# Moving the bookkeeping of a mixture-of-experts router by half a step to a step in a decoder layer's hand-written order

## The chip, the cores and the metric

The kernel runs on 1 core of one Trainium2 chip. Its time is the device time of one execution in microseconds (us). Before the change: 553.12 us, the median of 3 runs (552.07 to 553.45). A core has five engines with queues of their own, each of which works in order: TensorE (PE in the profile; PEld are its weight loads), VectorE (DVE), ScalarE (ACT), GpSimd (POOL), and SyncE (SP), which here only issues DMAs.

## The reference

One decoder layer on x (16 sequences of 128 rows, 256 wide), with a residual around each of three parts:

```python
x = x + attn(layernorm(x))          # latent attention: 16 heads, q of width 72, causal softmax,
                                    #   keys = values = layernorm(x) @ latent_w + latent_b
x = x + birwkv(layernorm(x), ctx)   # sigmoid(r) * (weighted sums of ctx, forth and back in time)
x = x + ffn(layernorm(x))           # 8 experts, the top two of each row, weighted
```

The last part takes logits (2048 rows by 8), picks the two largest of each row, forms the weights of the pair, and adds for each expert `weight * (silu(x @ w_gate.T) * (x @ w_up.T)) @ w_down.T` to the rows that chose it.

## The kernel before

The work is one list of steps, written out by hand. Steps 0 to 63 are the attention: step s is sequence b = s // 4 and head group s % 4 (4 heads of 16). Steps 64 and on are the experts' slots, one slot of 128 rows a step (36 slots, and 3 that are run only if needed).

An attention step issues the scores (L442), the row maxima on DVE (nm, L459), the exps on ACT (L467), and in the next step the reciprocal of the sums (rsum, L479, DVE) and the product with it (pr, L480, POOL). Two steps after its scores the probabilities are transposed (pt, L486), copied out by ACT (aT, L488) and multiplied by the values (py, L494). Query tiles of the next pair of sequences (pq, L404), the output projection (po, L520) and the second part's work for earlier sequences fill the step. I write nm(26) for the maxima issued in step 26, and pt(26) for the transposes issued in step 26; pr(24) is the product for the scores of step 24.

A step has five places: "pre", "A", "B", "C", "D" (L1243, L1246, L1259, L1278, L1283). `at(step, place, fn)` puts an extra piece of work into one. The manual schedule keeps this order, so the order of the places is the order in each engine's queue. "pre" follows the rsum and pr of the step before; "A" follows the transposes; "B" stands behind the new query matmuls and ahead of the values; "C" stands behind the copies of the query tiles, and in a slot behind `up`; "D" is last, in a slot behind `turn` and `down`.

Pieces that the change and the prediction touch:

- `route(r)` (L666): the routing of four sequences, a generator in five parts and then eight scatters. Part 1 (L681 to L691) and part 2 (L684 to L689) find the first and the second expert on DVE; part 3 (L694 to L700) makes sel, d and kp on DVE and one exp on ACT; part 4 (L705 to L723) counts with five small matmuls pf on TensorE and makes the weights g on DVE and the entries on POOL; part 5 (L726 to L737) makes the places on DVE. The scatters (L741) are issued by POOL. Rounds 0, 1 and 2 begin with sequences 3, 7 and 11; round 3 has an order of its own.
- The mix (`mix_1`, `mix_2`, L602 to L609) reads the transposed sums pw from a PSUM bank that pt needs, and POOL adds the result to x. Then statistics (L305), shift (nb_c, L320), the row (L625), its transposes (px, L640), their copy x2T (L645), and the logits pl (L652).
- The scans (L545, L562) and POOL's products kv, S and sums S<-S,bw (L536, L537, L557) belong to the second part. `residual` (L573) ends the first.
- `first_table(0)` (L869) is made after sequence 7 in six parts from the counts pc (L758): whole, share, and four parts of `table` (L773). SP then loads the table (L842) and its list entries. `last_table` (L883) is made in seven parts during slots 11 to 13.
- A slot j gathers its rows (xr, L912), copies two weights (w, L934: one on ACT, one on DVE), turns xr (pxr, L942) into xT (L944), and makes two products s and pu (L980), sl (L990, ACT), hT (L992, DVE), pd (L1002) and y (L1013, DVE), which POOL adds to the output by a DMA (L1018). In the step of slot j the order is: w of j+1, s and pu of j, hT of j, place "C", xT of j+1, pd and y of j-1, place "D".

Of the kernel before, what the change touches and what calls it, by code (L numbers as in the profile page):

```python
# [19 lines left out]
B = 16  # L20
T = 128
N = B * T
C = 256
# [56 lines left out]
def decoder_kernel(  # L80
# [950 lines left out]
    def at(step, place, fn, *args):  # L1031
        plan.setdefault((step, place), []).append((fn, args))
# [107 lines left out]
    for b in range(B):  # L1140
        s = NHG * b
        if b + 1 < B:
            at(s + 2, "pre", load_ctx, b + 1)
        at(s + 1, "C", wkv_exps, b)
        at(s + 2, "B", wkv_back, b)
        at(s + 3, "A", wkv_back_add, b)
        at(s + 4, "B", wkv_forth, b)
        at(s + 5, "A", wkv_forth_add, b)
        at(s + 5, "B", project, b, (0, 1))
        at(s + 6, "B", project, b, (2, 3))  # L1150
        at(s + 6, "C", rest_values, b)
        at(s + 7, "B", project, b, (4, 5))
        at(s + 7, "C" if b < B - 1 else "B", project, b, (6, 7, NP))
        for name, (step, place) in {B - 2: last_but_one, B - 1: last}.get(b, usual).items():
            at(s + step, place, stages[name], b)
        if b < E:
            for k in range(3):
                at(s + 11 + k, "C", load_expert, b, k)
        if b % RB == RB - 1:
            r = b // RB  # L1160
            parts = ((13, "B"), (13, "C"), (14, "B"), (15, "B"), (15, "C"))
            if b == B - 1:
                parts = ((12, "B"), (12, "D"), (13, "B"), (13, "D"), (14, "B"))
            for step, place in parts:
                at(s + step, place, route_part, r)
            for k in range(2 * RB):
                if b < B - 1:
                    at(s + 16 + k, "A", route_part, r)
                else:
                    at(s + 14 + (k + 1) // 3, "CDA"[(k + 2) % 3 if k > 1 else k], route_part, r)  # L1170
        if b + 1 in FIRST_B:
            i = FIRST_B.index(b + 1)
            parts = [(18 + k, "C") for k in range(6)]
            if i:
                parts = [(18, "C"), (20, "D"), (21, "B"), (21, "D"), (22, "D"), (23, "D")]
            for step, place in parts:
                at(s + step, place, table_part, i, first_table, i)
            for k in range(0, S1[i], 2):
                at(s + 24 + k // 2, "C", list_slots, min(2, S1[i] - k))
        if b == B - 1:  # L1180
            for k in range(7):
                at(s + 15 + k // 3, "ABD"[k % 3], table_part, "2", last_table)
            for k in range(0, S2, 4):
                at(s + 17 + k // 4, "C", list_slots, min(4, S2 - k))
            for k in range(4):
                at(s + 20 + k, "B", table_part, "3", very_last)
            for k in range(0, S3, 4):
                at(s + 24 + k // 4, "C", list_slots, min(4, S3 - k))
# [153 lines left out]
```

## Time and profile before

| what | us |
|---|---|
| median of 3 runs | 553.12 |
| the profiled execution, its own time | 554.7 |
| its span, first to last instruction | 553.0 |
| TensorE busy | 512.8 (93%) |
| DVE, ACT, POOL busy | 330.6, 329.3, 327.1 |
| mean granted TensorE clock | 0.984 |

The page's second part cuts the span into 40 equal slices and gives the busy tenths of each:

```profile
PE   4889999999999999999998989999989999989990
...
DVE  3354776687887678888769776555644533333330
ACT  1788998898797888888986873434313232313200
POOL 5356647564787774697646976454875454541532
PEclk9999999999999999999998999999989999999996
```

The attention lasts for about 24 slices, to some 320 us, with DVE and ACT at seven to nine tenths; in the slots after it TensorE is nearly alone. PEclk is the granted TensorE clock: it was at half of full speed from 296.8 to 300.2 us and from 406.0 to 409.4.

The timeline's rows give start, length, engine, line, operation, tiles and shapes, and in brackets how long the engine had been idle before it and what ended that. The ends of matmuls are modelled. Waits name the one who came last.

### The profile page before, as it was taken

What the parts mean: (1) busy time and instruction counts of PE and PEld (TensorE: products, weight loads), DVE (VectorE), ACT (ScalarE), POOL (GpSimd) and SP (SyncE); (2) the same over time, 40 slices, a digit from 0 to 9 for tenths busy, and PEclk for the clock granted to TensorE, in tenths of its full rate; (3) what the DMA queues carried; (4) which work ended last, traced back from release to release, by engine and by line L of the source; (5) the groups of instructions that cost most, each with busy time, mean ns of one, the idle gap of its engine ahead of it and who ended that gap; (6) DMA issues with size and microseconds to landing.
All of it is one profiled execution on the core that took longest, in us unless ns stands there. A gap on an engine that the chain in (4) does not pass through costs nothing. (4 is left out here: it accounts for less than half of the span.)

```text
span 553.0 us, 10138 instructions
## 1 busy us (share of the span) xinstructions
PE 512.8 (93%) x3272; PEld 439.2 (79%) x3272; DVE 330.6 (60%) x831; ACT 329.3 (60%) x953; POOL 327.1 (59%) x379
## 2 busy tenths in 40 slices
PE   4889999999999999999998989999989999989990
PEld 3768787887777887877875679989979999989980
DVE  3354776687887678888769776555644533333330
ACT  1788998898797888888986873434313232313200
POOL 5356647564787774697646976454875454541532
PEclk9999999999999999999998999999989999999996
DMA  5432245364365545131121113232234232325321
GB/s 149 98 88 67 70 133 170 121 198 120 110 182 133 170 130 178 41 98 37 52 79 56 40 53 66 38 65 45 40 40 51 48 51 47 51 47 173 58 30 19
DMA packets 39662, 47.59 MB, mean 86 GB/s; under 512 B 14136, under 2 KB 31416, under 8 KB 39576
## 3 DMA queue, kind: packets, MB, share of 16 engines
q1 hardware_dynamic: 30106, 37.20, 23.0%
q0 software_dynamic: 7936, 9.51, 11.2%
q8 instruction: 28, 0.46, 0.3%
q10 hardware_dynamic: 1566, 0.21, 0.3%
q14 instruction: 26, 0.21, 0.2%
HBM read 28.22 MB, written 13.31 MB: 75 GB/s over the span
## 5 line engine op out<-in xcount | busy, mean ns | idle before, releaser
L467 ACT ACTIVATE pr<-s,nm 128x128 f32<-128x128 f32 x256 | 90.7, 370 | 9.7 <-DVE nm L459 9.5
L480 POOL TENSOR_TENSOR pr<-pr,rsum 128x512 f32<-128x512 f32 x64 | 75.7, 1183 | 33.5 <-DVE rsum L479 25.6
L990 ACT ACTIVATE sl<-s 128x512 f32<-128x512 f32 x36 | 21.5, 598 | 120.7 <-PE s L980 104.9
L1018 POOL DMA_INDIRECT acc<-y,en x28 | 47.5, 1697 | 60.4 <-DVE y L1013 29.8
L442 PEld LDWEIGHTS s<-kvT,q 72*128 72x128 f32 x512 | 65.7, 191 | 18.7 <-issue 12.6
L980 PEld LDWEIGHTS s<-xT,w 128*128 128x128 f32 x576 | 70.5, 195 | 9.4 <-issue 6.7
L980 PE MATMUL s<-xT,w 128*128 128x128 f32 x576 | 72.0, 279 | 5.4 <-DVE xT L944 2.3
L520 PE MATMUL po<-outw_sb,yP 128*128 128x256 f32 x288 | 74.4, 385 | 0.6 <-DMA yP<-yd 0.6
L442 PE MATMUL s<-kvT,q 72*128 72x128 f32 x512 | 70.5, 279 | 3.2 <-DMA q<-qr 2.2
L980 PE MATMUL pu<-xT,w 128*128 128x128 f32 x576 | 70.5, 276 | 0.0
L992 DVE TENSOR_TENSOR hT<-sl,pu 128x512 f32<-128x512 f32 x36 | 24.7, 687 | 74.1 <-PE pu L980 56.9
L1002 PE MATMUL pd<-wall,hT 128*128 x288 | 68.0, 379 | 0.0
L494 PE MATMUL py<-aT,kvN 128*72 128x512 f32 x128 | 66.4, 600 | 1.6 <-ACT aT L488 1.3
L980 PEld LDWEIGHTS pu<-xT,w 128*128 128x128 f32 x576 | 67.7, 193 | 0.0
L404 PE MATMUL pq<-xnT,wq_sb 128*128 128x256 f32 x256 | 65.3, 387 | 0.0
L520 PEld LDWEIGHTS po<-outw_sb,yP 128*128 128x128 f32 x288 | 54.0, 193 | 13.1 <-issue 5.2
L459 DVE TENSOR_REDUCE nm<-s 128x4 f32<-128x512 f32 x64 | 43.6, 682 | 30.5 <-PE s L442 30.5
L1002 PEld LDWEIGHTS pd<-wall,hT 128*128 128x128 f32 x288 | 52.0, 190 | 5.6
L467 ACT ACTIVATION_READ_ACCUMULATOR pr<-s,nm 128x1 f32 x256 | 53.0, 207 | 0.0
L488 ACT COPY aT<-pt 128x512 f32<-128x512 f32 x64 | 37.2, 581 | 26.0 <-PE pt L486 24.6
L404 PEld LDWEIGHTS pq<-xnT,wq_sb 128*128 128x128 f32 x256 | 46.2, 195 | 5.0 <-issue 0.2
L912 POOL DMA_INDIRECT xr<-xn,en x36 | 37.4, 1040 | 13.3 <-issue 7.6
(172 smaller groups left out, 877.8 us busy)
## 6 DMA issues: line engine op xcount, KB each, us to landing
wall<-in_wg_dram SPq DMA_DIRECT2D x8, 512.0 KB
wall<-in_wu_dram SPq DMA_DIRECT2D x8, 512.0 KB
wall<-in_wd_dram SPq DMA_DIRECT2D x8, 512.0 KB
q<-q SPq DMA_DIRECT2D x16, 224.0 KB
yP<-yB SPq DMA_DIRECT2D x32, 112.0 KB
cx<-in_cx_dram SPq DMA_DIRECT2D x16, 128.0 KB
acc<-x SPq DMA_DIRECT2D x16, 128.0 KB
xn<-row SPq DMA_DIRECT2D x16, 128.0 KB
```

The lines of the kernel that those rows point to most:

```text
L404: nc.tensor.matmul(pq[:, :GT], w[:, c, :], xnT[g][:, c, :], start=(c == 0), stop=(c == NC - 1))
L442: nc.tensor.matmul(ps[:, j, :], q[g, hg][0:L, j, ts(i, T)], kvT[g][:, ts(i, T)], start=False, stop=(j == HG - 1), skip_group_check=n >= 2,)
L459: nc.vector.tensor_reduce(nm, ps, AX.X, ALU.max, negate=True)
L467: nc.scalar.activation(pr[:, j, :], ps[:, j, :], AF.Exp, bias=nm[:, j : j + 1], accum_out=sums[:, j : j + 1],)
L480: nc.gpsimd.tensor_mul(pr, pr, rsum.unsqueeze(2).to_broadcast([P, HG, T]))
L488: nc.scalar.copy(aT, pt)
L494: nc.tensor.matmul(py[:L], kvN[g][:, ts(i, L)], aTs.pop((b, hg)), start=True, stop=True)
L520: nc.tensor.matmul(pos[b][:, :C], yP[b][:, i, :], outw_sb[:, i, :], start=(i == 0), stop=(i == NP))
L912: nc.gpsimd.indirect_dma_start(out=xr, out_offset=None, in_=xn2[0 : t["rows"], :], in_offset=bass.IndirectOffsetOnAxis(ap=entries[j][:, 0: ...
L980: nc.tensor.matmul(o[:, ts(f, P)], w[:, c * F + f * P : c * F + (f + 1) * P], xT[:, c, :], start=(c == 0), stop=(c == NC - 1),)
L1002: nc.tensor.matmul(pd[:, :C], hT[:, f, :], wall[:, bass.ds(e, 1), WD0 + f * C : WD0 + (f + 1) * C], start=(f == 0), stop=(f == NF - 1),)
L1018: nc.gpsimd.indirect_dma_start(out=acc if j < SF + S2 else out2, out_offset=bass.IndirectOffsetOnAxis(ap=en[:, 1:2], axis=0), in_=y, in_of ...
```

## The change

Three sets of places are moved; no operation is added or dropped.

```diff
         if b % RB == RB - 1:
             r = b // RB
-            parts = ((13, "B"), (13, "C"), (14, "B"), (15, "B"), (15, "C"))
+            parts = ((14, "B"), (14, "C"), (15, "B"), (15, "C"), (16, "pre"))
             if b == B - 1:
                 parts = ((12, "B"), (12, "D"), (13, "B"), (13, "D"), (14, "B"))
...
             i = FIRST_B.index(b + 1)
-            parts = [(18 + k, "C") for k in range(6)]
+            parts = [(19 + k, "C") for k in range(6)]
             if i:
                 parts = [(18, "C"), (20, "D"), (21, "B"), (21, "D"), (22, "D"), (23, "D")]
...
             for k in range(7):
-                at(s + 15 + k // 3, "ABD"[k % 3], table_part, "2", last_table)
+                at(s + 15 + k // 3, "BCD"[k % 3], table_part, "2", last_table)
```

In the order of the built kernels this becomes: in rounds 0, 1 and 2 parts 1 and 2 stand behind the mix and the next step's maxima instead of ahead of them; part 3 one set of maxima later, with its exp behind the next step's exps on ACT; part 4's matmuls behind py instead of ahead of po; part 5 behind the next rsum. In step 46's place the counts pc stand in step 47, behind the transposes pxn, and each later part of the first table a step later. In slot 11 the share of the last table goes from ahead of the copy of w to between hT and xT; in slot 12 five operations (L801 to L807) do the same. POOL and SP keep their order; ACT's only move is the exp.

## The prediction

> **What bounds the kernel now.** I read the page first, then who TensorE waited for, then the busy time of stretches, then the timeline at each place the diff touches. Times are from the span's start.
>
> ```profile
> PE 512.8 (93%) x3272; PEld 439.2 (79%) x3272; DVE 330.6 (60%) x831; ACT 329.3 (60%) x953; POOL 327.1 (59%) x379
> ```
>
> TensorE sets the pace; a change counts only through TensorE's waits. The waits of PE:
>
> ```profile
> PE s L980 <- DVE xT L944: 2.3, 2, 2.1
> PE pt L486 <- POOL pr L480: 2.3, 2, 1.5
> ...
> PE pt L486 <- DVE m L684: 1.3, 2, 0.7
> ...
> PE pc L758 <- ACT q L410: 1.0, 1, 1.0
> ```
>
> All four stand where the diff moves something. In the timeline they are 0.68 and 0.67 us in routing rounds 0 and 1 (137.8, 215.1), 1.50 in round 2 (295.3), 1.04 at the first table (239.0), 2.14 in the last table (405.6); a fifth, pf after ACT q, is 0.2 twice. Next the stretches (columns: length, busy time of PE, PEld, DVE, ACT, POOL, granted clock, DMA):
>
> ```profile
> 132.40:148.60 16.20, 15.32 (x91) 12.27 (x90) 14.18 (x45) 12.89 (x43) 9.28 (x14) 1.00 0.36 129
> 293.37:296.79 3.42, 1.92 (x19) 1.73 (x17) 3.32 (x13) 2.44 (x11) 1.99 (x4) 1.00 0.30 83
> 296.79:300.20 3.41, 3.41 (x8) 2.13 (x9) 3.34 (x8) 2.52 (x11) 3.41 (x5) 0.50 0.00 0
> ```
>
> Over a whole routing round VectorE (DVE) is 14.18 of 16.20 us busy: there it is nearly a second bound. The last two rows show that the 1.50 us wait is followed by 3.41 us at half clock. Then the timeline of round 0:
>
> ```profile
> 137.79 0.77 POOL L609 TENSOR_TENSOR x<-x,r 128x256 f32<-128x256 f32 x1 [4.14 <-DVE m L684]
> 137.79 0.63 PE L486 MATMUL pt<-ident,pr 128*128 128x128 f32 x4 [0.68 <-DVE m L684]
> 138.00 0.60 DVE L687 TENSOR_TENSOR oh<-oh,rev 128x32 f32<-128x32 f32 x1
> ...
> 149.06 0.68 DVE L459 TENSOR_REDUCE nm<-s 128x4 f32<-128x512 f32 x1
> ...
> 149.65 0.41 DVE L645 COPY x2T<-px 128x256 f32<-128x256 f32 x1
> ...
> 151.36 0.51 PE L652 MATMUL pl<-rw_sb,x2T 128*128 128x8 f32 x4
> ```
>
> L687 takes 0.19 us alone and 0.60 here: it ends as the POOL operation that began before it ends. L689, L694 and L711 do the same (0.43, 0.88, 0.87). Reductions, and operations with an operand in PSUM, do not. So a routing operation behind a POOL product costs up to that product's length (0.75 to 1.05). x2T ends 1.3 us before pl needs it: that is the slack of nm(28), which precedes it.
>
> **Rounds 0 and 1, worked on round 0 (steps 25 to 28; scores begin at 131.88, 136.01, 140.84, 147.65).** Removed: the seven operations of part 1 (1.32 us) ahead of the mix at 133.67. The mix ends at 136.32 instead of 137.64, so pt(26) is free at once: TensorE gains 0.68, and 0.21 more as pf no longer follows pq directly. nm(26) comes at 137.15 instead of 139.49, with DVE idle for 0.35.
>
> Added: the same seven now stand behind nm(26), from 137.8. The earlier mix releases POOL's x, kv, S and pr (0.75, 0.72, 0.72, 1.05) back to back from 136.5 to 139.8, so L681, L686 and L687 wait for one product each: part 1 takes 2.7 instead of 1.3. Statistics and scan (2.0) and part 2 (1.1) follow; nm(27) is at 143.45 (now 143.50). So nothing is won there, but part 3, done by then before, is still to do. sel (L694) waits behind pr of step 26 until 144.7, L697 behind S<-S,bw (L557) until 145.7, kp is ready at 146.3. ACT's L700 has ended its exps and mask at 146.3 and runs at 146.4; the new wait is that L711 stands right behind, on DVE, until 146.7 (behind it: g, rsum(27), part 5, nm(28)). g and rsum follow until 147.5; then part 5, 1.28 plus about 0.8 since L730 meets pr(27), until 149.4; residual and statistics 1.2. nm(28) is at 150.6, **1.57 later than 149.06**.
>
> On TensorE pf comes to its place at 144.1 and waits for sel until 144.7; s(28) starts at 147.2, 0.47 ahead. But x2T ends at 151.63, so pl waits until 151.8 and s(29) is 0.4 late. ScalarE (ACT) runs its exps 1.5 late in steps 28 to 30, the mix of step 29 follows 1.35 late, and POOL's pr(29) (159.61 to 161.56, with pt(31) just behind it at 161.61) ends near 162.9. **Cost +1.35 per round**, after the 0.88 won. TensorE has no spare time to win it back. Ends: −0.9 (all stalls gone, nothing new), +1.6. The scatters L741 stand behind rs_b at 149.98 and their place is ready at 149.5: free.
>
> **The first table with round 1.** pc waits for ACT q because both banks hold pq(5) and pq(6) of a step with two tiles; a step later one tile is made and the bank is free: −1.04. But pt(47), now at 240.19, needs pr(45), which ended at 238.82 and comes 1.35 later with round 1, at 240.2. So the 1.04 only hides in the delay of round 1: the pair costs +0.3 (pc's own 0.25 moved behind pt, little else), up to 0.65 if the yP load of step 47 is late too; I take **+0.5**, ends −1.9 and +1.0. Of the other parts, the last stands in step 52 ahead of rsum(52) and delays it from 266.9 to 268.0, ahead of nm(53) at 268.4; SP's load of the table is at 268.7, so the list DMAs on SP behind it stay. Without that cover 1.0.
>
> **Round 2.** No query tiles remain, a step is about 4 us, and DVE has 3.32 of 3.42 filled. The wait of 1.50 and the half clock go. The same chain then gives nm(59) at 296.6 (now 297.75), sel behind pr(58) at 297.95, while TensorE stands before pf from 296.0: a **new wait of 2.0**. nm(60) follows at 303.9 (303.06 now), pl waits 1.05 for x2T, and py(61), held by ACT, starts at 308.35 (307.82). **+0.55**, ends −2.7 and +1.6.
>
> Here a rule and a row differ. The Trainium skill, "TensorE: Matmul & The Clock Gate", section "Why this matters for your kernels", puts the drop to half clock at gaps of about 3 us. In this trace a wait of 1.50 was enough, in a stretch filled with transposes and pf. By the rule the old wait has cost 1.5 and the new one of 2.0 costs only itself; by the row the old one has cost 1.5 + 1.7, and the new one may bring another half-clock stretch, which lies where TensorE waits 0.6 + 1.05 anyway. I follow the row; the end of this sum is set by ACT's chain either way.
>
> **The last table.** Slot 11: the five share operations (393.83 to 394.68) lie now in idle time ahead of hT. They go between hT (to 396.77) and xT, which ends at 398.04 instead of 397.10; s at 397.75 moves by 0.44. Slot 12: five operations (1.2 us) leave the place before the copy of w and go between hT and xT.
>
> ```profile
> 404.41 0.69 DVE L992 TENSOR_TENSOR hT<-sl,pu 128x512 f32<-128x512 f32 x1 [1.13 <-PE pd L1002]
> ...
> 405.01 0.42 DVE L944 COPY xT<-pxr 128x256 f32<-128x256 f32 x1
> ...
> 405.58 3.35 PE L980 MATMUL s<-xT,w 128*128 128x128 f32 x16 [2.14 <-DVE xT L944]
> ```
>
> DVE was free for hT at 403.3; it waited on to 404.4 for TensorE's signal, though pu shows its end at 401.5. Elsewhere hT starts 0.11 after pu. If the signal is as late again, s comes at 407.3: +1.7. If not, hT is at 402.25, the five operations to 404.15, s at 404.7, and the half clock after it goes: −0.9 − 1.7 = −2.6. The nearest row is the 0.11 of the other slots, but the profiled execution (554.7, span 553.0) is 1.6 above the median of the runs, so they have probably lacked that signal's lateness already. Against the median I take **0**. Parts moved from A to B, where slots have nothing between, change no order.
>
> **Sum.** 1.35 + 0.5 + 0.55 + 0 = +2.4: 555.4 of span, 557.1 as profiled; on the median 553.1 + 2.4 = **555.5**.
>
> **Rivals.** First: the stalls go and DVE keeps up. For it: each wait removed is on TensorE, and DVE is free for a while ahead of rounds. Against it: 14.18 of 16.20. Sum −0.9 − 0.9 − 1.04 − 1.0 + 0.2 = −3.6: 549.5. It decides if nm(28) is no later than 150.3, the slack before pl. Second: half of it, DVE's part 1 slips between POOL's products: rounds near 0, table −1, round 2 about +0.5, last table +0.2: 553, no change. My forecast is the slower one; its mechanism is DVE's queue between nm(27) and nm(28), price 1.57, and its opposite is the first rival.
>
> **Numbers.** Slower chain 0.54, the even case 0.23, stalls gone 0.23. What can be told from no change is 0.3% (1.7 us). The range reaches from 550.0 (most of the rival's case) to 558.0 (last signal late again, both rounds at their upper ends). The slower case's own range is 554.0 to 558.0.
>
> **What would show it.** Right: nm(28) 1 to 2 us later against s(25) than the present 17.2; pl waiting for x2T; pf waiting for DVE; pt after the round waiting for POOL pr; pc without wait, and a new wait at pt in the same step. Wrong: no wait at pl, or L687 and L694 at 0.19; then the first rival holds. In the last table, hT 0.11 after pu or late again.

## The result, and the profile after

| | median | runs |
|---|---|---|
| before | 552.27 us (550.71 to 553.45) | 7 |
| after | 555.38 us (554.51 to 555.93) | 7 |

The ratio is 1.0045, with a 95% interval of 1.003 to 1.006: after is slower, by 3.1 us where 2.4 were forecast. Yet the two profiled executions have almost the same span, 553.0 and 552.8. Their traces show why: the profile of before holds one accident of 2.8 us. The profiled execution took 554.7 us, longer than each of the seven runs of before, so these probably lacked it. First the page of after, its line of busy times:

```profile
PE 512.3 (93%) x3272; PEld 437.8 (79%) x3272; DVE 334.4 (60%) x831; ACT 328.6 (59%) x953; POOL 327.1 (59%) x379
```

TensorE does the same work; VectorE (DVE) is busy for 3.8 us more with the same 831 instructions. So they last longer on the average. Who TensorE waited for in after (columns: sum in us, times, longest):

```profile
PE pf L705 <- DVE sel L694: 3.3, 3, 1.8
PE pt L486 <- POOL pr L480: 2.7, 3, 0.9
...
PE pl L652 <- DVE nr L581: 1.0, 2, 0.6
```

The waits of before for `m` and for ACT `q` are gone from the list. In their place stand pf (0.72, 0.71, 1.84 in the three rounds), pl (0.42, 0.57) and pt behind POOL's pr in rounds 0 and 1 (0.88 each). The timeline of DVE in round 0 follows. The first line is nm(25) of before, all others are of after: nm(25), then nm(26), and so on to nm(28). In after s(25) lies 0.66 us earlier than in before.

```profile
133.06 0.69 DVE L459 TENSOR_REDUCE nm<-s 128x4 f32<-128x512 f32 x1 [0.83 <-PE s L442]
```

```profile
132.40 0.69 DVE L459 TENSOR_REDUCE nm<-s 128x4 f32<-128x512 f32 x1 [0.83 <-PE s L442]
...
136.50 0.69 DVE L459 TENSOR_REDUCE nm<-s 128x4 f32<-128x512 f32 x1 [0.55 <-PE s L442]
...
138.26 0.97 DVE L687 TENSOR_TENSOR oh<-oh,rev 128x32 f32<-128x32 f32 x1
...
143.33 0.74 DVE L694 TENSOR_TENSOR sel<-oh 128x32 f32<-128x32 f32 x1
...
144.09 1.08 DVE L698 TENSOR_TENSOR kp<-ab,m 128x32 f32<-128x32 f32 x1
...
145.95 0.23 DVE L711 TENSOR_TENSOR d<-d,kp 128x64 f32<-128x64 f32 x1 [0.25 <-ACT d L700]
...
146.83 1.15 DVE L730 TENSOR_TENSOR d<-oh,pos 128x32 f32<-128x32 f32 x2
...
149.87 0.68 DVE L459 TENSOR_REDUCE nm<-s 128x4 f32<-128x512 f32 x1
```

nm(26) starts 0.8 us behind the mix now and 1.9 in before. But L687, L694, L698 and L730, of 0.2 to 0.3 us each, last 0.7 to 1.15. (L694 was long in before too, 0.88, and so were L711, 0.87, and L689, 0.43; the last two are short now.) nm(28), the last line, comes 17.47 us after nm(25); in before, where it starts at 149.06, it was 16.00. What follows on TensorE and POOL in after:

```profile
150.94 0.61 PE L652 MATMUL pl<-rw_sb,x2T 128*128 128x8 f32 x4 [0.42 <-DVE nr L581]
...
160.24 1.95 POOL L480 TENSOR_TENSOR pr<-pr,rsum 128x512 f32<-128x512 f32 x1
...
162.24 0.66 PE L486 MATMUL pt<-ident,pr 128*128 128x128 f32 x4 [0.88 <-POOL pr L480]
```

To see where time went I take the start of each step on TensorE (its first scores; in the slots, sl) in two traces, and see how their distance changes over a stretch. Against the first profile of before, in us:

| stretch | after | routing alone | first table alone | last table alone | before again |
|---|---|---|---|---|---|
| round 0 (steps 25 to 40) | +1.28 | +1.26 | 0.00 | +0.14 | -0.02 |
| round 1 and first table (40 to 53) | +0.94 | +0.95 | -0.51 | +0.01 | 0.00 |
| steps 53 to 57 | +0.31 | +0.04 | +0.60 | +0.05 | +0.31 |
| round 2 (57 to slot 0) | +0.70 | +0.70 | -0.01 | -0.37 | +1.64 |
| slots 11 to 15 | -2.80 | -2.86 | -2.85 | -2.81 | -2.85 |

The four columns on the right are experiments. The last one is the kernel before once more, so it tells what chance does: nothing in rounds 0 and 1, 0.3 at the load of yP, 1.6 in round 2. Chance can also reach round 0: x4 below, whose attention has the order of before, stands at +0.90 there, nearly all of it in step 35, where TensorE waits 0.56 for a load of yP.

Round 2 needs care. All nine traces with the routing of before have the wait of 1.5 us there, and the row follows the half clock behind it: -0.37 and -0.36 where none came (e3, x1), -0.01 to +0.02 with 3.4 us of it (the first profile, e2, x3), +1.63 to +1.65 with 6.8 us (e4, e9, x2, x4). The five traces with moved routing (after, e1, e6, e7, e8) lie at +0.65 to +0.73, three of them with 3.4 us of half clock and two with none. So the +0.70 of after holds against the first profile; against the others it is between -0.95 and +1.07.

The last row is the accident: the other five traces, three of them with the old order of the last table, all lack it. Against a trace of before without it (e4) the last table's move is worth 0.05.

### The profile page after: what moved, and what is told of

The parts are those of the page before. It is cut to its first block, busy times and chain, and to the rows that moved or that the text cites. A ratio compares the mean times of both kernels' runs of the same rounds, so it can differ in the third digit from the quotient of the medians.

```text
span 552.8 us, 10138 instructions
## 1 busy us (share of the span) xinstructions
PE 512.3 (93%) x3272; PEld 437.8 (79%) x3272; DVE 334.4 (60%) x831; ACT 328.6 (59%) x953; POOL 327.1 (59%) x379
## 5 line engine op out<-in xcount | busy, mean ns | idle before, releaser
L980 PEld LDWEIGHTS s<-xT,w 128*128 128x128 f32 x576 | 69.2, 192 | 8.3 <-issue 5.7
L980 PE MATMUL s<-xT,w 128*128 128x128 f32 x576 | 70.8, 276 | 4.0 <-DVE xT L944 2.1
```

The source lines that it names most:

```text
L980: nc.tensor.matmul(o[:, ts(f, P)], w[:, c * F + f * P : c * F + (f + 1) * P], xT[:, c, :], start=(c == 0), stop=(c == NC - 1),)
```

## The experiments

Kernels of a group ran on the same chip beside runs of before, whose median was 551.85 in the first group (e1 to e4), 554.40 in the second (e6 to e9) and 554.01 in the third (x1 to x4). Each group had a chip of its own, so only ratios are compared from one group to another.

| kernel | median | ratio to before (95%) |
|---|---|---|
| e1, routing alone | 554.07 | 1.0052 (1.0034 to 1.0070) |
| e2, first table alone | 551.46 | 0.9999 (0.9988 to 1.0010) |
| e3, last table alone | 551.29 | 0.9994 (0.9982 to 1.0006) |
| e4, before again | 551.80 | 0.9999 (0.9985 to 1.0013) |
| e6, part 5 later still | 556.72 | 1.0042 (1.0025 to 1.0059) |
| e7, parts 1 and 2 at their old places | 558.68 | 1.0074 (1.0050 to 1.0097) |
| e8, after without six products | 574.81 | 1.0359 (1.0339 to 1.0379) |
| e9, before without six products | 571.05 | 1.0283 (1.0261 to 1.0304) |
| x1, a version meant to beat both | 553.95 | 0.9970 (0.9948 to 0.9991) |
| x2, last table spread | 554.66 | 1.0015 (0.9986 to 1.0044) |
| x3, first table and its list loads | 552.37 | 0.9963 (0.9947 to 0.9979) |
| x4, last table alone again | 556.79 | 1.0040 (1.0023 to 1.0057) |

**Which of the three moves costs: e1 to e4.** e1 is before with only this line changed:

```diff
-            parts = ((13, "B"), (13, "C"), (14, "B"), (15, "B"), (15, "C"))
+            parts = ((14, "B"), (14, "C"), (15, "B"), (15, "C"), (16, "pre"))
```

> The routing's move alone. My theory (DVE's chain between nm(27) and nm(28) sets the cost): about +1.3 us in round 0, +1.0 to +1.5 in round 1, where the counts pc are still in step 46 and wait for ACT q again (1.0 us), +0.4 to +0.7 in round 2: 2.6 to 3.5 us above before, ratio 1.005 to 1.006. Rival (the last table's new places between hT and xT carry the cost, the routing is about even): within 1 us of before.

Measured: 0.52% (2.9 us; by the interval 1.9 to 3.9). The rival falls: the routing alone carries the cost of the whole change. In step 46 pc waited 1.35 for ACT q (expected: 1.0), and pt behind it no longer waited.

```diff
-            parts = [(18 + k, "C") for k in range(6)]
+            parts = [(19 + k, "C") for k in range(6)]
```

> The first table's move alone. My theory: pc no longer waits for ACT q (1.04 us), pr(45) has ended at 238.8 of before, so nothing takes the place of this wait: 1.0 us below before (0 to -1.1). In the pair with the routing this gain is hidden in the routing's own delay. Rival (the table's later parts delay rsum(52) and SP's list DMAs, and cost time themselves): 0.3 to 1 us above before.

Measured: no change. This missed; neither theory holds as put. The trace shows 0.51 won by step 49, not 1.0, and 0.60 given back at step 56. At step 48 TensorE now waits 0.28 at pl, for kvT from DVE, where before had no wait: this is a part of what is missing from the 1.0. At step 56 it waits for the load of yP, where before had 0.29:

```profile
281.41 0.70 PE L520 MATMUL po<-outw_sb,yP 128*128 128x256 f32 x2 [0.88 <-DMA yP<-yd]
```

At step 53 TensorE was 0.47 earlier than in before, and the load of yP (L514) went out no earlier (279.41, in before 279.29). x3 below follows this up.

```diff
-                at(s + 15 + k // 3, "ABD"[k % 3], table_part, "2", last_table)
+                at(s + 15 + k // 3, "BCD"[k % 3], table_part, "2", last_table)
```

> The last table's move alone. My theory: about 0 against the median of before (from s of slot 11 to s of slot 13 12.2 us, as after has it; before 12.3 where hT of slot 12 comes when DVE is free, 13.4 as profiled, with the half clock behind it). Rival (this move carries the cost): s of slots 11 and 12 delayed by 0.5 each and nothing given back, 1 to 2 us above before.

Measured: no change, as my theory had it. (x4 below is the same kernel in the third group; there it was slower.)

> The kernel before, unchanged, for a second profile of it: ratio 1.000 within 0.002. If hT of slot 12 waits again for TensorE's signal 2.9 us after the recorded end of pu, the lateness belongs to the order of the kernel before, and the last table's move takes it away in each execution; if it comes at about 403.3 (DVE free), it belonged to one execution. The same for the half clock after it and after the wait at 295.3.

Measured: 0.9999. Its slot 12 in the timeline:

```profile
404.72 0.68 DVE L992 TENSOR_TENSOR hT<-sl,pu 128x512 f32<-128x512 f32 x1
...
405.88 0.79 PE L980 MATMUL s<-xT,w 128*128 128x128 f32 x5 [0.92 <-DVE xT L944]
```

hT has no wait at all (it follows the copy of w on DVE), and s waits 0.92, not 2.14. So the late signal in the first profile of before does not come with its order alone. The wait of 1.49 at round 2 and half clock after it are there again, for 6.8 us this time.

**What in the routing costs: e6 to e9.** e6 is after, with

```diff
+            if r < 2:
+                parts = parts[:4] + ((16, "D"),)
...
-                    at(s + 16 + k, "A", route_part, r)
+                    at(s + (17 if r < 2 else 16) + k, "A", route_part, r)
```

> The kernel after, with part 5 of rounds 0 and 1 two places later still (step 28, place D, behind nm(28), x2T and the scan) and their scatters one step later; all else as after. My theory (what costs is DVE's work ahead of nm(28)): nm(28) comes at 148.0 to 148.5 instead of 149.9, pl doesn't wait, pt(31) doesn't wait for pr(29), and with the stalls of before gone too rounds 0 and 1 give 1.3 to 2.2 each: 2.5 to 4.4 below after, within 1.3 of before on either side (ratio 0.998 to 1.002). Rival (the wait of pf for sel, 0.7, and the exp behind the exps on ACT set the cost): as after, 3 above before.

Measured: 0.42% above before, outside what I expected of the whole. In rounds 0 and 1 the mechanism did as expected. DVE's timeline in e6:

```profile
148.62 0.68 DVE L459 TENSOR_REDUCE nm<-s 128x4 f32<-128x512 f32 x1
...
150.94 0.17 DVE L726 TENSOR_TENSOR pos<-pf,ebase 128x32 f32<-128x32 f32 x1
151.14 0.29 DVE L730 TENSOR_TENSOR d<-oh,pos 128x32 f32<-128x32 f32 x2
```

nm(28) is 15.64 after nm(25) and part 5 stands behind it. Neither pl nor pt(31) waits; pf still does, 0.71. By the step starts round 0 is at 0.00 against before (after: +1.28), and round 1 with the first table at -0.53, which is what e2's move gives alone. So pf's wait is no more than what the old stalls cost, and what a round costs on top goes through the late nm(28). The rest of e6's time lies further down: 0.66 at the load of yP, 0.67 in round 2, which is as in after, and 1.73 in slots 11 to 15, at the last table (see x4).

e7 is after, with

```diff
-            parts = ((14, "B"), (14, "C"), (15, "B"), (15, "C"), (16, "pre"))
+            parts = ((13, "B"), (13, "C"), (15, "B"), (15, "C"), (16, "pre"))
```

> The kernel after, but parts 1 and 2 of the routing at their places of before; parts 3, 4 and 5 moved as in after, both tables as in after. My theory: part 3 behind nm(27) and part 5 behind rsum(27) make nm(28) late by themselves, and the wait of pt for the mix (0.67) is back: rounds 0 and 1 cost as in after or up to 0.5 more each, 3 to 4 us above before. Rival (parts 1 and 2 behind POOL's products carry the cost, 1.4 us a round): 0 to 1 above before.

Measured: 0.74%, 4.1 us, which is what my theory gave; but its reason was wrong. In the step starts round 0 costs 0.56 (after 1.28), and round 1 with the table 0.23 (0.94). Leaving parts 1 and 2 where they were takes off 0.7 a round. The rest of e7's 4.1 us is mostly the last table once more (1.77 in slots 11 to 15). Its nm(28) stands 16.76 behind nm(25).

e8 is after, and e9 before, with

```diff
-        nc.gpsimd.tensor_mul(pr, pr, rsum.unsqueeze(2).to_broadcast([P, HG, T]))
+        if NHG * b + hg not in (25, 26, 27, 41, 42, 43):
+            nc.gpsimd.tensor_mul(pr, pr, rsum.unsqueeze(2).to_broadcast([P, HG, T]))
```

> The kernel after without POOL's product pr for the scores of steps 25, 26, 27, 41, 42 and 43 (their probabilities stay unnormalised; this part of the computation is left out). My theory (a routing operation waits until a POOL product that began before it has ended): L687 of part 1 falls from 0.97 to about 0.2, sel from 0.74 to 0.2 or to what another product leaves, L730 from 1.15 to 0.29; nm(28) comes 1 to 2 us earlier and rounds 0 and 1 lose their cost: 2 to 4 below after. Rival (DVE's own work sets nm(28)): nm(28) within 0.3 of after, the time within 1 us of after.

> The control: the kernel before without the same six products. My theory: it has little to win there, since nm(28) has slack before pl in it: 0 to 1.0 below before. Rival (the product is a cost of its own in both kernels): as much below before as the run without the products is below after.

The whole times say nothing here: with six products missing other rows choose other experts, and the slots at the end differ (in both, TensorE waits 6.3 us there for a gather). The attention is untouched by that. DVE in e8, where each operation's line number is one higher than in after:

```profile
139.12 0.19 DVE L688 TENSOR_TENSOR oh<-oh,rev 128x32 f32<-128x32 f32 x1
...
142.19 1.11 DVE L688 TENSOR_TENSOR oh<-oh,rev 128x32 f32<-128x32 f32 x1
...
144.33 0.18 DVE L695 TENSOR_TENSOR sel<-oh 128x32 f32<-128x32 f32 x1
...
146.79 0.22 DVE L712 TENSOR_TENSOR d<-d,kp 128x64 f32<-128x64 f32 x1 [1.54 <-ACT d L701]
...
147.66 0.29 DVE L731 TENSOR_TENSOR d<-oh,pos 128x32 f32<-128x32 f32 x2
...
149.84 0.68 DVE L459 TENSOR_REDUCE nm<-s 128x4 f32<-128x512 f32 x1
```

The three operations named shrink to their own 0.19, 0.18 and 0.29. Two things stand in for part of it: S<-S,bw now begins earlier and holds part 2's L688 (L687 in after) for 1.11, and the operation behind ACT's exp waits 1.54 (in after 0.25), since ScalarE takes the exps of its step first. nm(28) is 16.58 behind nm(25): 0.89 earlier than in after. On TensorE round 0 costs 0.37 and round 1 with the table 0.03, that is 0.91 less each. So nm(28) moved, against the rival's theory, but less than the 1 to 2 that I had expected, and a part of the cost stays. In the control e9 the same omission changes the two rounds by -0.02 and +0.01, and its nm(28) stays at 16.00. So POOL's six products cost after 0.9 a round, and before nothing; that they do so through DVE is read from the lengths of the three operations.

**Can both be beaten: x1 to x3, and the last table again.** x3 is e2 with the list loads of the first table in place D:

```diff
-                at(s + 24 + k // 2, "C", list_slots, min(2, S1[i] - k))
+                at(s + 24 + k // 2, "D" if i == 0 else "C", list_slots, min(2, S1[i] - k))
```

> The first table's move alone, with its list loads in place D. Theory (in the move alone the 0.5 won at pc was given back at step 56, where TensorE waited 0.88 for the load of yP, issued behind list loads on SP): that wait falls to 0 to 0.3, and 0.5 to 1.1 below before. Rival (the load of yP is bound by its store, not by SP's queue): the wait stays 0.6 to 0.9, and the time is that of before.

Measured: 0.9963, 2.0 us below before by the ratio. SP's queue in e2 and then in x3:

```profile
278.01 0.87 SPq L863 DMA_DIRECT2D en<-lists  x2
...
279.41 0.42 SPq L514 DMA_DIRECT2D yP<-yd  x1
```

```profile
277.53 0.38 SPq L514 DMA_DIRECT2D yP<-yd  x1
279.23 0.91 SPq L863 DMA_DIRECT2D en<-lists  x2
```

Measured from the start of step 53, the load of yP goes out 2.3 us sooner. In e2 three things stood ahead of it on SP: a load of the lists' start values (L842, TENSOR_LOAD, 1.08 us) and the two list loads (0.87 together); in x3 they are behind it. TensorE's wait of 0.88 is gone. The step starts give 1.07 up to step 57 against the first profile of before, as expected; the interval of the ratio is 1.2 to 2.9 us, so a rest of the 2.0 is not placed.

x2 is before with a part of the last table moved; x1 is x2 and x3 together.

```diff
-                at(s + 15 + k // 3, "ABD"[k % 3], table_part, "2", last_table)
+                step, place = ((15, "A"), (15, "B"), (15, "D"), (16, "A"), (16, "D"), (17, "A"), (17, "A"))[k]
+                at(s + step, place, table_part, "2", last_table)
```

> Before, with only L801 to L807 of the last table moved behind y of slot 12. Where hT of slot 12 waits only for DVE, it comes 1.0 to 1.7 earlier and slot 12 lasts 5.6 instead of 6.6: 1.0 below before. Where TensorE's signal for hT is late by 2.9 as in the first profile of before, nothing is won: 0.

> A version meant to beat both: routing as before; first table's parts one step down as in after, with its list loads in place D (behind the load of yP in SP's queue) instead of C; the last table's operations L801 to L807 behind y of slot 12 instead of ahead of its w. The sum of x3 and x2: 1.0 to 2.3 below before, ratio 0.996 to 0.998. Rival: the gains are taken up by the next wait down the line (ACT's chain in steps 57 to 63, TensorE's late signal in slot 12): within 0.5 of before.

x2 is inconclusive (0.9986 to 1.0044), x1 is below before but not shown better than x3. In both profiles the late signals of TensorE took the place of what was to be won: slot 12 lasts 7.2 and slot 13 8.8.

> The last table's move alone once more. If TensorE's signal for hT of slot 12 is on time in the profile: 0 against before, as in the first such run. If it is late again, as in the profiles of the third call: slot 12 lasts 9.1 instead of 7.8, and 1 to 2 above before.

(The profiles that this text speaks of are those of e6 and e7; "the first such run" is e3.) Measured: 1.0040, and the signal was late. Slot 12 in x4, then in after:

```profile
408.57 0.69 DVE L992 TENSOR_TENSOR hT<-sl,pu 128x512 f32<-128x512 f32 x1 [3.97 <-remote]
409.17 0.27 DVE L801 TENSOR_TENSOR past<-past,lead 128x112 f32<-128x112 f32 x1
...
410.29 0.42 DVE L944 COPY xT<-pxr 128x256 f32<-128x256 f32 x1
...
410.85 0.98 PE L980 MATMUL s<-xT,w 128*128 128x128 f32 x3 [4.02 <-DVE xT L944]
```

```profile
404.90 0.69 DVE L992 TENSOR_TENSOR hT<-sl,pu 128x512 f32<-128x512 f32 x1 [0.39 <-PE pu L980]
407.19 0.35 PE L980 MATMUL s<-xT,w 128*128 128x128 f32 x1 [0.44 <-DVE xT L944]
```

In after hT starts 0.11 behind pu and the five operations L801 to L807 cost TensorE 0.44. In x4 it starts 3.69 behind the recorded end of pu, and the five then stand fully on the path. (The ends of matmuls are modelled: a late signal can also mean that the products really ended later than recorded.) From s of slot 11 to s of slot 14, in us, in every profile with one of the two orders:

| order | signal on time | signal late |
|---|---|---|
| of before | 17.8 (e1, e2, e4) | 20.6 (first profile of before, e9), 19.1 (x3) |
| of after | 17.8 (after, e3) | 22.4 (e6, e7, e8), 24.3 (x4) |

So the last table's move is free where the signal is on time. Where it is late the move costs 1.8 in the second group (22.4 against 20.6) and 5.1 between the two profiles of the third (24.3 against 19.1); the median of x4 is 2.8 above that of before. All profiles of the first group were on time and all eight of the later two were late, and before itself was slower in these by 2.2 to 2.6 us. So the lateness goes with the group, that is with the chip or the time; no run separates the two, and what makes the signal late is not settled.

## Why the prediction was right, point by point

The direction, the rough size and the chain that the forecast named were right. That the median of 555.38 lies so near the forecast 555.5 is partly luck: the change was put 0.7 too small, and the median of before that it was added to, 553.12 from three runs, came out as 552.27 with seven. By its steps:

- **Rounds 0 and 1: forecast +1.35 in round 0, measured +1.28.** The chain came as written: part 1 lasts 2.7, sel ends when pr does, L730 meets pr(27), nm(28) is 1.47 late (forecast 1.57), pl waits 0.42, and pt(31) waits for pr(29). e8 with e9 shows 0.9 of it to be POOL's products pr; e6, where pf's wait is still there and nm(28) is early, shows the whole +1.28 gone. What I made of it for e7 was wrong, though: I put the whole cost on parts 3 to 5, and e7 puts 0.7 of it on parts 1 and 2, of which part 1 takes 2.7 us instead of 1.3. The row behind all this, operations on two operands in SBUF that end when a GpSimd product ends, agrees with the Trainium skill ("SBUF — State Buffer", section "Who interferes with whom": a DVE instruction with two SBUF inputs contends with a GpSimd instruction that reads SBUF, and the order of issue decides who waits); e8 is the test of it, 0.97 to 0.19 at L687. Reductions stay short: L688 takes 0.19 at 138.63 of before, in the middle of POOL's kv.
- **First table with round 1: forecast +0.5, measured +0.94.** The mis-sized term is the move of the table. It was put at -1.04 alone, as nothing was to take the wait's place; e2 shows -0.51, with a new wait of 0.28 at pl in step 48, and in the pair nothing of it is left: round 1 costs 0.95 with the table at its old place (e1) and 0.94 with it moved. A further 0.31 came at the load of yP. With the table moved and the list loads in place C this stretch costs 0.31 to 0.66 in five traces, with the table at its old place 0.00 to 0.31 in seven, so a part of it is the move's. That the list DMAs on SP "stay" was true of their times, but the load of yP behind them then did not follow TensorE, and e2 lost there what it had won.
- **Round 2: forecast +0.55, measured +0.70 against the first profile of before.** pf waited 1.84 for sel (forecast 2.0), and nm(60) came 0.70 later against the start of step 57 (forecast 0.84); pl waited for x2T in e1 (0.76, forecast 1.05) and not in after. e1 had the same wait at pf without half clock and also ended at +0.70, so after the move the end does not hang on the clock, as the forecast said. That it is ScalarE's chain is argued from the waits of py for aT (0.63 in both), not tested. In the old order the end does hang on the clock, from -0.37 to +1.65, so how near the size came is luck of the trace compared with.
- **Last table: forecast 0, ends -2.6 and +1.7.** All three were seen: -2.8 against the profile of before, 0.05 against before on time, +1.8 with both late in the second group. In the third it was more, 5.1 between two profiles, which the upper end did not allow for. The argument that the runs of before had mostly lacked the lateness fits their median of 552.27 in seven runs.
- **The rule of the clock.** The forecast followed the row (half clock after a wait of 1.50) against the rule of gaps of about 3 us (the Trainium skill, "TensorE: Matmul & The Clock Gate", section "Why this matters for your kernels"). It was right that shorter waits can bring it, but not that they always do: after the wait of 1.5 in round 2 half clock came in seven of nine traces of the old order, and not in e3 and x1, nor in e7, where pt has the same wait. The cost of the old half clock was mis-sized: the sum by the row takes 1.7 for its 3.4 us, but e3 and x1, without it, are only 0.37 faster in this stretch.
- **The rivals.** That the stalls go and DVE keeps up had nm(28) by 150.3 as its condition. Put on the times of before (s(25) at 131.88), nm(28) of after comes at 150.53, 0.2 too late for it. e6 meets the condition and gives no gain in round 0 either: of the 0.88 saved at pt and pf, 0.71 goes into pf's new wait, and by step 29 nothing is left. So this rival's -0.9 a round was wrong too.

Against the first profile of before the steps add up to 1.28 + 0.94 + 0.31 + 0.70 = 3.2 at the end of the attention, near the 3.1 of the medians. Against e4, which had 6.8 us of half clock in round 2, the same sum is 1.3. The granted clock suggests that most runs of before were more like the first: e4's profiled run has 0.983, and of the 35 runs of before in its group five have 0.982 and the others 0.985 or more (an estimate, since other stretches at half clock count in it too). How many runs had the longer half clock or a late signal is not known, since few were profiled; that is the open part of the sum. What is shown without it is that the routing's move alone costs 2.9 us by the medians (e1), and that in rounds 0 and 1 its cost goes with nm(28) (e6).

## What to carry to other kernels

A wait of the bottleneck engine that is removed by delaying small operations on another engine is only won if that engine has the time later: follow its queue to the next operation that the bottleneck needs (here nm(28)), and count each small operation on two operands in SBUF that meets a GpSimd product at up to the length of the product (here 0.2 us alone and up to 1.1). Where a move wins at one place, look for the next transfer that does not move with it; here list loads ahead of the load of yP in SP's queue ate the gain, and with these behind it the table's move gave 0.4% over the kernel before (x3; 0.2% to 0.5%). And one profile is one execution: compare the places of a gain in a second trace of the unchanged kernel before it is believed.

## What the runs showed of the hardware

- Half clock is not decided by the wait alone. The same wait of 1.84 at pf was followed by half clock for 3.41 us in after and by none in e1; the wait of 1.49 at pt by 6.8 us of it in e4 and by none in e3. Apart from the beginning and the end of the span it came in stretches of 3.41, 6.83 or (in e8 and e9) 10.24 us in all traces.
- The readers of TensorE's products can start up to 4.0 us after the recorded ends of the matmuls (sl in slot 13 of x1), where 0.04 to 0.11 is usual. I saw this in slots 12 and 13: in the first profile of before, in none of after and e1 to e4, and in all eight of the two later groups, e9 with the old order among them. In eight of these nine profiles half clock begins soon after it (in x3 it does not); the trace doesn't show why.
